# Four graph layers in one kernel: the attention layer in runs of two turns, PSUM as eight equal tiles, and closing steps per chunk

## Chip, cores and metric

The kernel runs on one core of a Trainium2 chip. The metric is the device time of one execution in microseconds (us); lower is better. The times are medians of several runs of the same program.

## What is computed

A graph of 4096 nodes with 64 features each, and a dense 0/1 matrix `adj` of 4096 x 4096, goes through four layers. Each has a layer norm and relu in front (`h`) and adds its result to `x`.

```python
# layer 0: weighted sums over neighbours, weights from a running count in each row of adj
x = x + (w(adj) @ (h @ W0) + b0)
# layer 1: attention masked by adj; q, k, s are "lorentz" linear maps of h
att = adj * sigmoid((2 + 2 * (qm @ k.T)) / att_scale + att_bias)
support = att @ s
x = x + support / sqrt(clip(abs(-inner(support)), 1e-8))
# layer 2: two gated steps (GRU), m = adj @ (g @ W)
r = sigmoid(i_r + h_r); z = sigmoid(i_z + h_z); n = tanh(i_n + r * h_n)
g = relu((1 - z) * n + z * g)
# layer 3: hyperbolic mean: num = adj @ (gamma * X), den = adj @ (gamma - 1),
# then scaling by tanh(alpha * 0.5 * artanh(|num / den|)), logmap, relu, expmap
```

## The kernel before

The nodes are cut into 32 blocks of 128 (`NB`), and the output nodes into four quarters `q` of 1024 (`NQ`), each of two halves `c` of 512 columns. `adj` is kept in SBUF in fp8, as tiles `A8[q][i]` for block pairs `i`. Each layer runs over the quarters, and inside a quarter over all 32 blocks, two blocks (one pair) to a turn.

**Order of the work.** Each engine executes its instructions in the order in which the program issues them. The streams of TensorE (`stream0`, `stream1`, `layer2`, `layer3`) are written out by hand. The small steps around them are Python generators (`post0`, `pre1`, `post1`, `post2a`, `post3` and others) that yield one instruction at a time. `Weave` holds a rough cost book of the engines; at each `weave.draw()` it issues those steps that should be ready by then, from the first two pieces of its list (`width`). `weave.until` and `weave.finish` issue steps until a result exists. `book_pe` is the planner's cost of a matmul; it charges a change between full and partial tiles of the array. All instructions of VectorE and ScalarE are issued by one helper, line 781, and all plain matmuls by line 976, so they are told apart here by the names of their tiles.

**PSUM.** There are four tiles of one bank (512 fp32 columns, `one`, line 820) and two of two banks (`two`, line 823). `weave.take` books a tile and `free` gives it back. Steps have an argument `kind` that says which of the two they use.

**Layer 1.** `weigh(q, i, c)` (line 1322) multiplies keys with queries for a pair of blocks and a half of 512 columns. The two blocks lie on the two halves of the partitions, so their score matmuls use array tiles of 64 x 128 side by side. One sigmoid of 1024 columns on ScalarE takes them from PSUM to a `sig` tile in SBUF (pool `b4`, six buffers, shared with the tiles `whole` of the check that `adj` has only zeros and ones). VectorE multiplies with the adjacency. `add` (in `stream1`, line 1345) sums over blocks with array tiles of 128 x 64 into two accumulators that live for a whole quarter. fp32 matmuls are recorded as two matmuls each, so two halves `c` of two blocks are eight records of scores and eight of sums to a turn. `stream1` issues the scores of turn i and then the sums of turn i - 1. In the first quarter it waits (`weave.until((1, ...))`) for the keys of each quarter, which `post0` and `pre1` of the last quarter still make. After the last sums of a quarter, `post1` takes its accumulators (`evac`: two copies `mt` on ScalarE, two adds on VectorE), transposes, normalises and makes the input of layer 2.

**Layer 3 and the end.** The output is made in eight chunks `u` of 512 nodes (four blocks, `CB`). `sum3` (line 1674) sums a chunk into two PSUM tiles, or one double tile in third place. `take3` (line 1737) copies it to `n65`. Chunks 0 to 2 get half their sums early, then 3 to 5 are completed, then 0 to 2, then 6 and 7 alone. `summed` (line 1729) starts `post3` for each three chunks together, and for 6 and 7 on their own. `post3` (line 1757) first has a group of seven steps for each chunk (sign, product, squares, `den`, sums of squares), then a chain of small steps for all chunks of the group, `artanh2` (line 1595) among them, and at its end the result `X` and its DMA. `preload` loads ScalarE's table for the next function ahead of its use.

Of the kernel before, what the change touches and what calls it, by code (L numbers as in the profile page):

```python
# [18 lines left out]
P = 128  # L19
D = 64  # L20
# [584 lines left out]
class Weave:  # L605
# [10 lines left out]
    def __init__(self):  # L616
        self.t = dict.fromkeys("PDAGS", 0.0)
        self.at, self.used = {}, {}
        self.banks = {1: [0.0] * 4, 2: [0.0] * 2}
        self.kind = {}  # L620
        self.work, self.back, self.width = [], [], 2
        self.late = 0.0
        self.quiet = False
        self.dma = 0.0
        self.busy = False
        self.table = None
        self.tiled = False
# [164 lines left out]
def fast_kernel(ctx: ExitStack, tc: tile.TileContext, t: dict, out: bass.AP, flag: bass.AP):  # L792
# [27 lines left out]
    def one(name):  # L820
        return weave.take(1, lambda: psp.tile([P, CW], F32, tag="one", name=name, bufs=4))

    def two(name):
        return weave.take(2, lambda: psp.tile([P, 2 * CW], F32, tag="two", name=name, bufs=2))

    def bank(kind, name):
        return one(name) if kind == 1 else two(name)[:, :CW]
# [136 lines left out]
    def book_pe(o, lhsT, rhs, passes):  # L964
        k, m, n = lhsT.shape[0], math.prod(lhsT.shape[1:]), math.prod(rhs.shape[1:])
        tiled = k < P or m < P
        dur = max(0.42e-3 * n * passes * (0.5 if tiled else 1.0) * (0.5 if k < P and m < P else 1.0), 0.09)
        if passes > 1 and not tiled:
            dur += 0.05 if passes == 2 else 0.075
        weave.book("P", dur + ((0.18 if passes == 4 else 0.115) if tiled != weave.tiled else 0.0), names(lhsT, rhs), names(o))  # L970
        weave.tiled = tiled
# [16 lines left out]
    def transpose4(src, kind, dst):  # L988

        def run():  # L990
            ps = bank(kind, "ps_t")
            for j in range(4):
                turn4(ps[:, j * P:(j + 1) * P], src[:, 2 * j:2 * j + 2, :].rearrange("p t d -> p (t d)"))
            return ps
        ps = yield PE([src], run, 0.6, [kind])
        yield AC.activation(dst, ps, AF.Copy)
        free(ps)

    def linear4(fm, weights, kind):

        def run():
            ps = bank(kind, "ps_l")
            for j in range(4):
                mm(ps[:, j * P:(j + 1) * P], fm[:, j * P:(j + 1) * P], weights)
            return ps
        return (yield PE([fm], run, 0.9, [kind]))
# [59 lines left out]
    def to_nm(a, kind):  # L1066

        def run():
            ps = bank(kind, "ps_n")
            for j in range(4):  # L1070
                turn4(ps[:, j * P:(j + 1) * P], a[:, j * P:(j + 1) * P])
            return ps
        ps = yield PE([a], run, 0.7, [kind])
        return blocks(ps)
# [30 lines left out]
    def checks():  # L1105
# [18 lines left out]
        def run():  # L1124
            ps = two("flag_ps")
            mm(ps[:1, :1], odds, ones)
            return ps
        ps = yield PE([odds], run, 0.3, [2])
# [3 lines left out]
    def stream0():  # L1132
# [56 lines left out]
        for q in range(NQ):  # L1189
            cnt[:] = [two(f"cnt{c}")[:, :CW] for c in (0, 1)]  # L1190
# [44 lines left out]
    def post0(q, acc):  # L1235
# [3 lines left out]
        ps = blocks((yield from linear4(a, w("w0"), 1)))  # L1239
# [31 lines left out]
    def pre1(q, X):  # L1271
# [5 lines left out]
        yield from transpose4(h, 1, fm)  # L1277
        hs = b2("hs")
        ps = yield from linear4(fm, w("w1"), 1)
# [6 lines left out]
        yield from transpose4(S1[q], 1, fm)  # L1286
# [19 lines left out]
        yield from transpose4(y, 1, kT[q])  # L1306
        DONE.add((1, q))
        qT = b2("qT", (P, CW))
        yield from transpose4(yq, 1, qT)
# [12 lines left out]
    def weigh(q, i, c):  # L1322

        kb = kT[i // 4][:, (i % 4) * P:(i % 4 + 1) * P]
        ps = two("score").rearrange("p (j n) -> p j n", j=2)
        for j in range(2):
            half = slice(j * D, (j + 1) * D)
            mm(ps[:, j, :], kb[half, :], qd[q][c][half, :])
        g = b4p.tile([P, 2, CW], F32, tag="b4", name="sig")
        S_.activation(g, ps, AF.Sigmoid, bias=att_add, scale=att_mul)  # L1330
        free(ps)
# [7 lines left out]
    def begin1():  # L1339

        for c in (0, 1):
            ahead.append(weigh(0, 0, c))
            weave.draw(False)

    def stream1():
# [11 lines left out]
        def add_behind():  # L1357
            q, i, gs = behind.pop()
            for c in (0, 1):
                add(c, q, i, gs)  # L1360
                weave.draw(weave.quiet)
            if i == NB // 2 - 1:
                weave.finish()
                weave.add(post1(q, acc[:], 1 if q < NQ - 1 else 2))
                acc.clear()

        for q in range(NQ):
            for i in range(NB // 2):
                if q == 0 and i % (QB // 2) == 0:
                    weave.until((1, i // (QB // 2)), DONE)  # L1370
                weave.quiet = (1, NQ - 1) not in DONE
                weave.late = 2.0 if weave.quiet else 1.0
                gs = ahead[:] if (q, i) == (0, 0) else []
                for c in range(len(gs), 2):
                    gs.append(weigh(q, i, c))
                    weave.draw(c == 1 or weave.quiet)
                if behind:
                    add_behind()
                behind.append((q, i, gs))
                if i == 8:  # L1380
                    load1(q + 1)
# [4 lines left out]
    def post1(q, acc, kind):  # L1386
# [4 lines left out]
        ps = yield from to_nm(a, kind)  # L1391
# [19 lines left out]
        yield from transpose4(g, kind, gT)  # L1411
# [82 lines left out]
    def load_gates(step):  # L1494
# [6 lines left out]
        def run():  # L1501
            ps = two("ps_g")
            mm(ps[:, :3 * D], m[:, :2 * D], m[:, 2 * D:])
            return ps
        ps = yield PE([m], run, 0.4, [2])
# [7 lines left out]
    def gates(q, step):  # L1513
# [4 lines left out]
        rz, ih = [None], [None]  # L1518
        assert ("gates", step) in DONE

        def news():

            ih[0] = two("ih")
            for c, (x, m) in enumerate(((lo, hi), (hi, lo))):
                o = lo if c == 0 else hi
                for own, half, i in ((x, 1, 2), (m, 0, 3)):
                    k = (4 * c + i) * D
                    mm(ih[0][o, half * CW:(half + 1) * CW], gw[own, k:k + D], mx[c][own, :])

        def gate(ps, half, i):  # L1530
            if ps[0] is None:
                ps[0] = two("rz")
            o = ps[0][:, half * CW:(half + 1) * CW]
            for c in (0, 1):
                k = (4 * c + i) * D
                mm(o[lo if c == 0 else hi, :], gw[:, k:k + D], mx[c])

        yield PE(mx, lambda: gate(rz, 0, 0), 0.9, [2, 2])
        yield PE(mx, news, 0.9, [2])
        r = b2("r", (P, CW))  # L1540
        yield AC.activation(r, rz[0][:, :CW], AF.Sigmoid, bias=gate_b[:, 2 * step:2 * step + 1])
        yield PE(mx, lambda: gate(rz, 1, 1), 0.9)
        yield DV.scalar_tensor_tensor(r, ih[0][:, CW:], gb[:, 5:6], r, op0=ALU.add, op1=ALU.mult)
        yield DV.tensor_tensor(r, r, ih[0][:, :CW], ALU.add)
        free(ih[0])
        z = b2("z", (P, CW))
        yield AC.activation(z, rz[0][:, CW:], AF.Sigmoid, bias=gate_b[:, 2 * step + 1:2 * step + 2])
        free(rz[0])
# [6 lines left out]
    def post2a(q):  # L1555
        x = yield from gates(q, 0)
        yield AC.activation(x, x, AF.Relu)
        ps = yield from to_nm(x, 1 if q < NQ - 1 else 2)
# [4 lines left out]
    def post2b(q):  # L1563
        o = yield from gates(q, 1)
        DONE.add(("gates", q))
        kind = 1 if q < NQ - 1 else 2

        def run():
            ps = bank(kind, "ps_o")
# [3 lines left out]
        ps = yield PE([o], run, 0.6, [kind])  # L1573
        yield DV.scalar_tensor_tensor(X[q], blocks(ps), 0.0, X[q], op0=ALU.max, op1=ALU.add)
        free(ps)
        yield from pre3(q, kind)
# [18 lines left out]
    def artanh2(x, between=()):  # L1595
# [4 lines left out]
        r = stat("at", nb)  # L1600
        yield DV.tensor_scalar(r, xc, -1.0, 1.0, op0=ALU.mult, op1=ALU.add)
        q = yield from recip(r)
        yield DV.scalar_tensor_tensor(q, xc, 1.0, q, op0=ALU.add, op1=ALU.mult)
        yield AC.activation(q, q, AF.Ln)
# [7 lines left out]
        for c in ARTANH_POLY[2:-1]:  # L1612
            yield DV.scalar_tensor_tensor(p, p, 2.0 * c, x2, op0=ALU.add, op1=ALU.mult)
        yield DV.scalar_tensor_tensor(p, p, 2.0 * ARTANH_POLY[-1], xc, op0=ALU.add, op1=ALU.mult)
# [6 lines left out]
    def pre3(q, kind):  # L1621
# [3 lines left out]
        yield from transpose4(hn, kind, fm)  # L1625
        ps = yield from linear4(fm, w("w3"), kind)
# [47 lines left out]
    def sum3(u, place, lo, hi):  # L1674

        if u not in dst:
            v = [two("acc3")] if place > 1 else [one("acc3") for _ in range(2)]
            dst[u] = lo, [x.rearrange("p (k n) -> p k n", n=256) for x in v]
        start, v = dst[u]
        for d in range(CB):  # L1680
            o = v[0][:, d, :W3] if len(v) == 1 else v[d // 2][:, d % 2, :W3]
# [45 lines left out]
    group = []  # L1727

    def summed(u, parts3, alone=False):
        group.append((u, parts3))  # L1730
        if alone or len(group) == 3:
            weave.add(post3(group[:]))
            group.clear()
# [23 lines left out]
    def post3(parts3):  # L1757
# [6 lines left out]
        sgn, den, ss = stat("sgn", nb), stat("den", nb), stat("ss", 2 * nb)  # L1764
        part = [slice(i * CB, (i + 1) * CB) for i in range(len(parts3))]
        vs = [n65[:, :, :D] for u, (n65, al) in parts3]
        for h, v, (u, (n65, al)) in zip(part, vs, parts3):
            d = n65[:, :, D]
            yield DV.tensor_scalar(sgn[:, h], d, 0.0, 2.0, op0=ALU.is_ge, op1=ALU.mult)
            yield DV.scalar_tensor_tensor(v, rows(sgn[:, h]), -1.0, v, op0=ALU.add, op1=ALU.mult)  # L1770
            sq = b2("sq")
            yield AC.activation(sq[:, :CB, :], v, AF.Square)
            yield DV.scalar_tensor_tensor(sq[:, CB:, :], v, 0.0, v, op0=ALU.max, op1=ALU.mult)
            yield DV.tensor_scalar(den[:, h], d, -1.0, DEN_EPS, op0=ALU.mult, op1=ALU.max)
            yield DV.tensor_tensor(den[:, h], den[:, h], d, ALU.max)
            yield DV.tensor_reduce(ss.rearrange("p (k b) -> p k b", k=2)[:, :, h],
                                   sq.rearrange("p (k b) d -> p k b d", k=2), AX.X, ALU.add)
# [124 lines left out]
```

## Time and profile before

| | |
|---|---|
| median of the runs shown | 809.76 us (808.28 to 809.77) |
| the profiled execution, in all | 808.12 us |
| its span, first to last instruction | 806.1 us |
| TensorE, share of the span with matmuls | 96% |
| VectorE / ScalarE / GpSimd busy | 79% / 49% / 8% |
| mean granted TensorE clock | 0.992 |
| layer 0 / layer 1 / layers 2 and 3 / after the last matmul | about 0-239 / 234-493 / 493-788 / 788-806 us |

Busy time of matmuls includes a modelled end, so that a full PE row means that nothing was seen to wait. The last number in brackets of a line is the idle time of the engine ahead of it, with the instruction that ended it. PE is TensorE's matmuls, PEld its weight loads, DVE VectorE, ACT ScalarE, POOL GpSimd and SP the queue of SyncE.

### The profile page before, as it was taken

How to read it: one execution, taken by the hardware profiler on the slowest of the kernel's cores; microseconds unless marked ns; L12 is line 12 of the kernel's file. 1: busy time of each engine (PE TensorE's matmuls, PEld its weight loads, DVE VectorE, ACT ScalarE, POOL GpSimd, SP SyncE). 2: the span in 40 equal slices, each digit the busy share in tenths (PEclk: the TensorE clock that was granted, in tenths of full speed). 3: DMA queues.
4: the chain of work that ended last, by engine and by line, in shares of the span. 5: the costliest groups of instructions: out<-in, count | busy, mean ns of one | idle time of the engine just before them, and what ended most of it. 6: DMA issues, size and time to landing. Idle time of an engine off the chain costs nothing. (4 is left out here: it accounts for less than half of the span.)

```text
span 806.1 us, 12128 instructions
## 1 busy us (share of the span) xinstructions
PE 772.6 (96%) x4494; PEld 360.1 (45%) x4494; DVE 635.6 (79%) x1429; ACT 397.8 (49%) x613; POOL 60.6 (8%) x125
## 2 busy tenths in 40 slices
PE   5999999999999999999999999999999999999991
PEld 2334444544443323333333333444444444599991
DVE  6886867877778798888888887878788777776696
ACT  5655555566556556667666664122220245444332
POOL 3332232231000000000000000000000000000000
PEclk9999999999999999999999999999999999999996
DMA  9999999999601032004022016597888600000010
GB/s 221 152 177 191 215 163 211 202 180 205 186 26 40 0 103 85 23 8 124 0 66 66 0 51 229 193 338 240 292 307 280 216 7 20 2 1 2 2 41 17
DMA packets 43955, 98.40 MB, mean 122 GB/s; under 512 B 5104, under 2 KB 20464, under 8 KB 43888
## 3 DMA queue, kind: packets, MB, share of 16 engines
q1 hardware_dynamic: 25888, 78.98, 29.0%
q0 software_dynamic: 15840, 14.42, 19.1%
q10 hardware_dynamic: 2160, 4.14, 1.4%
q8 instruction: 37, 0.61, 0.3%
q14 instruction: 30, 0.25, 0.1%
HBM read 135.54 MB, written 5.24 MB: 175 GB/s over the span
## 5 line engine op out<-in xcount | busy, mean ns | idle before, releaser
L781 ACT ACTIVATE sig<-score,fatt_add,fatt_mul 128x1024 f32<-128x1024 f32 x128 | 148.3, 1200 | 85.2 <-PE score L976 84.1
L781 DVE TENSOR_TENSOR sig<-sig,A 128x1024 f32<-128x1024 f32 x128 | 151.6, 1222 | 38.2 <-ACT sig L781 37.5
L781 DVE SCALAR_TENSOR_TENSOR whole<-whole 128x1024 f32<-128x1024 f32 x128 | 153.0, 1219 | 6.7 <-DMA whole<-in_adjT 6.1
L781 ACT ACTIVATE w<-cnt 128x512 int16<-128x512 f32 x198 | 111.6, 595 | 88.4 <-PE cnt L976 83.7
L976 PE MATMUL score<-qd,kT 64*128 64x512 f32 x512 | 128.2, 617 | 0.0
L976 PE MATMUL acc<-sig,S 128*64 128x512 f32 x512 | 125.4, 606 | 1.5 <-DVE sig L781 1.4
L976 PE MATMUL acc<-A,hm 128*128 128x512 fp8e4 x512 | 115.9, 379 | 0.0
L976 PEld LDWEIGHTS <-hm 128*128 128x128 bf16 x768 | 73.4, 98 | 91.3 <-issue 9.8
L976 PE MATMUL cnt<-A,ftri 128*128 128x512 fp8e4 x256 | 98.0, 386 | 8.1 <-ACT A L781 8.1
L976 PE MATMUL cnt<-A,fupd 128*128 128x512 fp8e4 x248 | 95.4, 385 | 3.4 <-ACT w L781 0.9
L976 PE MATMUL acc<-S,A 128*128 128x196 bf16 x1024 | 88.2, 246 | 0.2 <-DVE mx L781 0.2
L976 PEld LDWEIGHTS <-A 128*128 128x128 fp8e4 x1024 | 87.1, 96 | 1.5 <-issue 1.2
L976 PEld LDWEIGHTS score<-qd,kT 64*128 64x128 f32 x512 | 43.7, 186 | 80.9 <-ACT sig L781 39.1
L976 PE MATMUL acc<-w,hm 128*128 128x512 bf16 x256 | 75.6, 379 | 0.0
L781 DVE TENSOR_SCALAR w<-cnt 128x512 int16<-128x512 f32 x58 | 40.1, 691 | 39.4 <-PE cnt L976 38.2
L860 POOL DMA_DIRECT2D A<-in_adjT x110 | 58.8, 536 | 133.1 <-DMA A<-in_adjT 132.3
L976 PEld LDWEIGHTS acc<-sig,S 128*64 128x64 f32 x512 | 30.4, 136 | 82.7 <-issue 38.8
L976 PEld LDWEIGHTS <-lo 128*64 128x64 bf16 x768 | 39.3, 109 | 51.2 <-issue 22.5
L976 PE MATMUL acc<-A,lo 128*64 128x512 fp8e4 x512 | 59.4, 381 | 0.0
L781 ACT ACTIVATE mt<-acc 64x512 f32<-64x512 f32 x32 | 18.9, 591 | 66.0 <-PE acc L976 65.5
L976 PEld LDWEIGHTS <-ftri 128*128 128x128 bf16 x256 | 24.8, 98 | 47.2 <-issue 20.3
L1659 POOL MEMSET S<- 128x4 bf16 x8 | 0.9, 115 | 533.6 <-PE ps_l L976 463.2
(185 smaller groups left out, 631.5 us busy)
## 6 DMA issues: line engine op xcount, KB each, us to landing
whole<-in_adjT SPq DMA_DIRECT2D x128, 512.0 KB, 6.9
A<-in_adjT POOLq DMA_DIRECT2D x110, 128.0 KB, 14.0
qd<-qs SPq DMA_DIRECT2D x16, 128.0 KB, 4.1
mx<-gs SPq DMA_DIRECT2D x16, 128.0 KB, 7.8
xT<-gs SPq DMA_DIRECT2D x8, 256.0 KB, 7.2
x<-in_x SPq DMA_DIRECT2D x6, 256.0 KB, 6.2
xs<-x SPq DMA_DIRECT2D x4, 256.0 KB, 6.0
qs<-qT ACTq DMA_DIRECT2D x4, 256.0 KB, 6.0
```

Source lines behind the costliest of these rows:

```text
L781: return fn(*args, **kw)
L860: nc.gpsimd.dma_start(A8[q][b // 2][:, b % 2, :], a)
L976: nc.tensor.matmul(o, lhsT, rhs, start=start, stop=stop, skip_group_check=True)
L1659: nc.gpsimd.memset(S3[q, c][:, :, 3 * e:], 1.0)
```

## The change

In layer 1 `stream1` goes over pairs of turns: the scores of two turns are issued one after the other, then the sums of the two turns before (turn i - 1 and turn i). `weigh` is split: `score` issues the matmuls, `weigh` the sigmoids and the product. The sigmoid of a chunk becomes two instructions of 512 columns, one for each bank. For the second turn of a pair, `weigh` is put off (`later`) until the first turn's sums have been issued half by half.

PSUM becomes eight tiles of one bank. All users of double tiles take two or four single ones; `kind` goes away. The order and shape of their matmuls stay. The planner's book tells the shapes of partial tiles apart.

In the closing part, the first group of steps of a chunk becomes `head3` and is started as soon as each chunk of a group of three is taken; `post3` runs it for the last one alone. `artanh2` takes the difference of two logarithms in place of the logarithm of a quotient.

```diff
-        self.banks = {1: [0.0] * 4, 2: [0.0] * 2}
+        self.banks = {1: [0.0] * 8}
...
-        tiled = k < P or m < P
+        tiled = (k < P) + 2 * (m < P)
...
-    def weigh(q, i, c):
+    def score(q, i, c):
         kb = kT[i // 4][:, (i % 4) * P:(i % 4 + 1) * P]
-        ps = two("score").rearrange("p (j n) -> p j n", j=2)
+        ps = several(("score", "score"))
         for j in range(2):
             half = slice(j * D, (j + 1) * D)
-            mm(ps[:, j, :], kb[half, :], qd[q][c][half, :])
+            mm(ps[j], kb[half, :], qd[q][c][half, :])
+        return ps
+
+    def weigh(q, i, c, ps):
         g = b4p.tile([P, 2, CW], F32, tag="b4", name="sig")
-        S_.activation(g, ps, AF.Sigmoid, bias=att_add, scale=att_mul)
-        free(ps)
+        for j in range(2):
+            S_.activation(g[:, j, :], ps[j], AF.Sigmoid, bias=att_add, scale=att_mul)
+            free(ps[j])
...
-        def add_behind():
-            q, i, gs = behind.pop()
+        def add_behind(more=()):
+            q, i, gs = behind.pop(0)
             for c in (0, 1):
                 add(c, q, i, gs)
+                if more:
+                    more.pop(0)()
                 weave.draw(weave.quiet)
...
+        def turn(q, i, later=None):
...
+            gs = ahead[:] if (q, i) == (0, 0) else []
+            for c in range(len(gs), 2):
+                ps = score(q, i, c)
+                if later is None:
+                    gs.append(weigh(q, i, c, ps))
+                else:
+                    later.append(lambda q=q, i=i, c=c, ps=ps: gs.append(weigh(q, i, c, ps)))
+                weave.draw(weave.quiet or c == 1)
+            behind.append((q, i, gs))
...
         for q in range(NQ):
-            for i in range(NB // 2):
...
+            for i in range(0, NB // 2, 2):
+                later = []
+                turn(q, i)
+                turn(q, i + 1, later)
+                while len(behind) > 2:
+                    add_behind(later)
+                for go in later:
+                    go()
+                if len(behind) > 1:
                     add_behind()
...
-        yield PE(mx, lambda: gate(rz, 0, 0), 0.9, [2, 2])
-        yield PE(mx, news, 0.9, [2])
+        yield PE(mx, reset, 0.9, [1] * 4)
+        yield PE(mx, news, 0.9)
...
-        r = stat("at", nb)
-        yield DV.tensor_scalar(r, xc, -1.0, 1.0, op0=ALU.mult, op1=ALU.add)
-        q = yield from recip(r)
-        yield DV.scalar_tensor_tensor(q, xc, 1.0, q, op0=ALU.add, op1=ALU.mult)
-        yield AC.activation(q, q, AF.Ln)
+        q, r = stat("at", nb), stat("ln", nb)
+        yield AC.activation(q, xc, AF.Ln, bias=ones)
+        yield AC.activation(r, xc, AF.Ln, bias=ones, scale=-1.0)
...
+        yield DV.tensor_tensor(q, q, r, ALU.subtract)
...
     def sum3(u, place, lo, hi):
-            v = [two("acc3")] if place > 1 else [one("acc3") for _ in range(2)]
+            v = several(("acc3", "acc3"))
...
     def summed(u, parts3, alone=False):
+        if not group:
+            n = CB if alone else 3 * CB
+            group.append((stat("sgn", n), stat("den", n), stat("ss", 2 * n)))
         group.append((u, parts3))
+        i = len(group) - 2
+        if not alone and i < 2:
+            weave.add(head3(i, parts3, *group[0]))
+            heads.append(weave.work[-1])
+            return
+        for piece in heads:
+            while piece in weave.work:
+                weave.issue(piece)
+        heads.clear()
+        weave.add(post3(group[1:], *group[0]))
+        group.clear()
...
     def post3(parts3, sgn, den, ss):
-        for h, v, (u, (n65, al)) in zip(part, vs, parts3):
...
+        yield from head3(len(parts3) - 1, parts3[-1][1], sgn, den, ss)
         yield from preload(AF.Ln)
         rd = yield from recip(den)
         n, r = yield from lengths(ss)
```

`head3(i, part3, sgn, den, ss)` holds the seven steps of the removed loop for one chunk, unchanged, with `i` as the chunk's place in the group.

## The prediction

> **What bounds the kernel now.** I read the busy table first, then the slices by stage, then layer 1 in order of time, then the end.
>
> ```profile
> PE 772.6 (96%) x4494; PEld 360.1 (45%) x4494; DVE 635.6 (79%) x1429; ACT 397.8 (49%) x613; POOL 60.6 (8%) x125
> ...
> 234.00:292.00 58.00, 54.74 (x240) 18.45 (x238) 46.18 (x83) 32.82 (x36) 0.00 (x0) 1.00 0.09 28
> ...
> 292.00:491.00 199.00, 198.98 (x854) 63.28 (x853) 168.74 (x229) 132.16 (x129) 0.00 (x0) 1.00 0.18 55
> ```
>
> The columns of the two stretches are length, then PE, PEld, DVE, ACT, POOL. TensorE is busy without a gap from 292 to 491, which is layer 1 after its first turns; only the first stretch, 234 to 292, has about 3 us of idle PE. So in layer 1 the sum of PE time is the time. VectorE is at 85% (168.74 of 199) and ScalarE at 66%.
>
> ```profile
> 419.76 1.99 PE L976 MATMUL score<-qd,kT 64*128 64x512 f32 x8
> 421.68 1.94 PE L976 MATMUL acc<-sig,S 128*64 128x512 f32 x8
> 423.55 1.99 PE L976 MATMUL score<-qd,kT 64*128 64x512 f32 x8
> 425.46 1.94 PE L976 MATMUL acc<-sig,S 128*64 128x512 f32 x8
> 427.33 1.99 PE L976 MATMUL score<-qd,kT 64*128 64x512 f32 x8
> ...
> 420.30 0.19 PEld L976 LDWEIGHTS score<-qd,kT 64*128 64x128 f32 x2 [0.24 <-issue]
> 420.73 0.19 PEld L976 LDWEIGHTS score<-qd,kT 64*128 64x128 f32 x2 [0.23 <-issue]
> ...
> 424.78 2.38 ACT L781 ACTIVATE sig<-score,fatt_add,fatt_mul 128x1024 f32<-128x1024 f32 x2 [1.32 <-PE score L976]
> ...
> 426.02 2.40 DVE L781 TENSOR_TENSOR sig<-sig,A 128x1024 f32<-128x1024 f32 x2 [0.16 <-ACT sig L781]
> ```
>
> One turn, 423.55 to 427.33, takes 3.785 us. Within a shape, pairs of matmuls follow each other every 0.43 us (weight loads 420.30, 420.73). A turn has eight pairs, 3.44 us. The other **0.35 us** goes into two changes of tile shape, 64\*128 for the scores and 128\*64 for the sums.
>
> ```profile
> 744.80 43.51 PE L976 MATMUL acc<-S,A 128*128 128x196 bf16 x510
> ...
> 750.75 0.88 DVE L781 TENSOR_TENSOR n<-n,acc 128x260 f32<-128x260 f32 x2 [4.93 <-ACT alpha L781]
> ...
> 788.94 0.61 DVE L781 TENSOR_TENSOR n<-n,acc 128x130 f32<-128x130 f32 x2
> ...
> 793.24 0.42 DVE L781 SCALAR_TENSOR_TENSOR sq<-n 128x256 f32<-128x256 f32 x1
> ...
> 800.29 0.42 DVE L781 TENSOR_TENSOR X<-X,n 128x256 f32<-128x256 f32 x1
> ```
>
> At the end PE stops at 788.3 and VectorE carries the rest: the last chunk's sums lie in SBUF at 789.55, but its squares start only at 793.24, because the chunk before it (u=6) is still being closed. VectorE stood idle for 4.93 us ahead of 750.75 and is nearly full from there on.
>
> [...] The trace has 1200 ns for 1024 columns with two pointers [...] and 686 ns for z, 512 columns with one pointer [...]
>
> **Layer 1, what it removes.** 64 turns become 32 pairs: two turns of scores, then two of sums, four changes become two. 0.35 us a pair, 32 pairs: 11.2 us at most.
>
> **Layer 1, what it adds.** (1) A chunk's sigmoid becomes two instructions of 512 columns. Half a chunk costs 1200 - 512 x 0.833 = 774 ns (the slope also follows from 595 ns for w, 512 columns, and 170 ns for alpha, 2 columns). ACT gets 128 x (2 x 0.774 - 1.2) = 45 us more duration, of which overlaps hide some; it had 66 us free in 292-491 alone and stays under 85%. So not a bound by itself.
>
> (2) Two turns of scores want eight banks, but the accumulators hold two. The fourth chunk must reuse the first chunk's banks. Let a pair begin at 0. The first matmul after a change takes 0.10 more (693 against 589 ns), so pairs start at 0, 0.53, 0.96, ...; the fourth chunk is due at 2.68. ACT starts 1.23 after the first scores (424.78 - 423.55). Its two halves end at 1.23 + 0.67 + 0.77 = 2.67, 0.67 being 0.77 less the overlap of 0.10 (two sigmoids in 2.30 us). With some 0.05 to hand over (ACT to DVE: 425.98 to 426.02) that is 2.72, and weights that cannot be loaded ahead cost 0.10: a wait of **0.15 us**. Bounds: 0 if half a chunk costs half (600 ns), 0.25 if nothing overlaps. Queued behind the waiting load on PE are the rest of the scores and both sums, so all of it counts. Kept: 0.35 - 0.15 = 0.20 a pair.
>
> (3) The six b4 buffers: four sigmoid chunks live and two for the adjacency check. The third chunk's sigmoid is put behind the first sums of the turn before, which end near 4.9; the last half ends near 7.7, the next pair's first sigmoid is due at 7.4 + 1.23 = 8.6. Behind it wait only its own product and sums, 2 us later. Cost 0, covered by that 0.9 us of ACT. The products: the first turn's sums need them at 5.4 and 6.3, they are ready about 4.0 and 5.3; one check (1.22 us) in front eats most of this cover, so I keep 0 to 0.1 a pair here for the range.
>
> (4) Where q changes, the old accumulators stay until both adds have run (the second of them started at 316.30, about 5 us after those sums at 309.56-311.43), so scores have four banks for a pair. Chunk three then waits for chunk one, chunk four for chunk two: up to 1.4 us; none if the adds are out early. I take 0.7, three times: 2.1. Each q has two groups of transposes that hold a bank (ps_n from 320.92 to the end of its copy, 323.45): 0 to 0.3, I take 0.15, six times: 0.9. Half of these come to lie between two turns of scores, where they cause two more changes: three times 0.2, 0.6. Sum 3.6.
>
> (5) In the first q, PE waits for the keys of the last quarter: 1.79 us idle ahead of the ps_t at 291.17. Six pairs, 1.2 us, run into this wait; I count half, 0.6 (0 if the chain of small steps does not move up, and it can lose 2 us if its steps queue behind longer runs of scores).
>
> Layer 1: 26 pairs x 0.20 = 5.2, + 0.6 - 3.6 = **2.2 us gained**; bounds -5 and +9.
>
> **PSUM in equal tiles elsewhere.** Same banks and same matmuls, so no PE time. A third-place unit is taken in two pieces, not one: 0.3 us more on DVE (four adds of 0.29 for two of 0.43), three times, off the path while PE runs to 788.3. Gates need four free banks at once, as they needed both double tiles. No DMA or queue entry is added; loads (SP) keep their place. Checks not done in a shorter layer 1 move to layer 2; the last one ran at 636.8, far from the end.
>
> **Closing steps.** The first step group of a chunk (sign, product, square, den, sums) is about 1.87 us of DVE (751.56 to 753.43). Today three such run together after the third chunk. Two of each three move ahead, the first two (3.7 us) into the 4.93 idle us before 750.75. Then the group 3, 4, 5 is out of the way near 765 and gives room for the next two. Group 0, 1, 2 starts at about 769.3, with one step group instead of three, and closes near 779 instead of 784.3. Chunk 6 is in SBUF at 779.0; it takes 1.9 + 5.8 us, done near 787, before chunk 7 at 789.55. So chunk 7 squares at about 790.2 instead of 793.24: **3.0 us**. Artanh: three small DVE steps and a Ln go (r, reciprocal, product: 0.2 each), one subtract and a Ln of 0.2 us on ACT come: 0.4 us less on DVE. ACT's table for tanh also loads earlier, since both Ln start right from the clipped value (796.78), ending about 0.4 sooner than 797.80. Together **3.5 us**, bounds 2 and 4.5.
>
> **Sum.** 2.2 + 3.5 = 5.7. The profiled execution had a span of 806.1 and 808.12 us in all; it lies 1.6 below the median of the runs shown, 809.76. I carry the difference over: 809.76 - 5.7 = 804.
>
> **Rivals.** A, the scores' banks cost nothing: halves fast enough and old accumulators gone. Layer 1 gives 9 to 10, all 13: **797**. For it: PE shows no bank wait today. Against: 774 ns for a half.
>
> B, the switches are saved, but waits for banks at the fourth chunk and at changes of q eat all: only the end gains, **806 to 808**. For it: my own margin is negative by 0.15.
>
> C, slower: **ScalarE becomes the pacer of the fourth chunk.** If the first chunk's second half ends 0.45 later (a side step of 0.6 us between, or a late start), each pair waits 0.60: 32 x 0.60 = 19.2 against 11.2 + 3.5: **814**. It decides from 0.46 us a pair. For it: every half has its own wait now. Against: of ACT's 132.16 us in 292-491 the sigmoids are 126 (52.5 turns x 2.4), so side work is 6 us only.
>
> D, slower too: the last quarter's gates in layer 3 (rz at 699.33) find three banks instead of four and wait for the first take at 710. The quarter is ready at 737 and used near 739, so up to 8 us of PE wait: **812**. For it: small margin. Against: today's double tiles are as scarce there.
>
> That shapes do not alternate less is excluded, since PE runs in program order.
>
> **Chances.** Forecast 0.40, A 0.22, B 0.20, C 0.10, D 0.08. B straddles the limit of 0.2% (1.6 us, about what a measurement of this kernel can tell from no change), and parts of C and D and of the forecast's low end meet there: faster 0.63, within 0.13, slower 0.24. The range 796 to 813 reaches from A to D and leaves most of C out. The forecast's own range is 800 to 808.
>
> **What would show it.** Right: score groups of 16 matmuls in a row, then sums of 16; a pair of turns near 7.4 us instead of 7.57; a half sigmoid near 770 ns; small PE waits on ACT at the fourth chunk; and 9 us instead of 12.4 from PE's end to the last X. Wrong: pairs of 7.22 (A) or above 7.6 (C), PE idle ahead of the last quarter in layer 3 (D), or the last chunk still squared 5 us after PE's end.

## The result, and the profile after

The changed kernel takes **806.82 us** (median of 13 runs, 806.41 to 807.29) against 808.22 us for the kernel before in the same comparison (13 runs, 807.83 to 809.77): ratio 0.9975, 95% interval 0.9967 to 0.9983 (the two medians alone give 0.9983). It is faster, by 1.4 us and not by 5.7. The kernel before has two groups of times, near 808.1 and near 809.6 us, for which the last section has a likely cause; its profiled execution (808.12) belongs to the first, so the stages below are compared with that one. The changed kernel's profiled execution took 807.01 us, span 805.1, mean clock 0.993.

Where the time went, from the first score, the first sums of layer 2 and of layer 3, and the end of the last matmul in each trace (us). The quarters of layer 1 run from first score to first score, the tail from the last matmul to the last output `X`:

| | layer 0 | q0, q1, q2, q3 of layer 1 | layer 1 | layer 2 | layer 3 | tail |
|---|---|---|---|---|---|---|
| before | 234.0 | 73.7, 61.7, 61.7, 63.8 | 261.0 | 199.4 | 93.9 | 12.4 |
| after | 234.2 | 70.5, 63.4, 63.5, 65.1 | 262.5 | 198.4 | 95.5 | 9.0 |

The tail gave the 3.4 us that it should. Layer 1, where 2.2 were to be gained, lost 1.5, and layer 3 lost 1.6.

The busy table of after, and its two stretches of layer 1 (length, then PE, PEld, DVE, ACT, POOL, clock):

```profile
PE 767.5 (95%) x4473; PEld 369.7 (46%) x4494; DVE 635.6 (79%) x1419; ACT 432.2 (54%) x756; POOL 61.6 (8%) x125
```

```profile
234.00:292.00 58.00, 56.73 (x257) 22.27 (x256) 48.73 (x88) 40.61 (x63) 0.00 (x0) 1.00 0.11 36
292.00:491.00 199.00, 192.63 (x832) 68.39 (x830) 172.87 (x236) 153.16 (x226) 0.00 (x0) 1.00 0.21 66
```

The stretch that was full before (198.98 of 199) now has 6.4 us of idle TensorE: there is less matmul time to do, and it is waited for. ScalarE is at 77%. An undisturbed pair, in the timeline (start, duration):

```profile
329.47 3.79 PE L973 MATMUL score<-qd,kT 64*128 64x512 f32 x16
333.19 3.65 PE L973 MATMUL acc<-sig,S 128*64 128x512 f32 x16
336.77 3.79 PE L973 MATMUL score<-qd,kT 64*128 64x512 f32 x16
...
330.63 2.79 ACT L781 ACTIVATE sig<-score,fatt_add,fatt_mul 128x512 f32<-128x512 f32 x4 [0.83 <-PE score L973]
334.31 2.79 ACT L781 ACTIVATE sig<-score,fatt_add,fatt_mul 128x512 f32<-128x512 f32 x4 [0.90 <-PE acc L973]
```

From 329.47 to 336.77 are 7.30 us, where two turns took 7.57: the saved changes are there. But not every pair looks like this. The waits of ScalarE and of the weight loads (us in total, times, longest) in after:

```profile
PEld acc L973 <- DVE sig L781: 26.1, 42, 1.8
...
ACT sig L781 <- DVE whole L781: 25.2, 18, 2.3
```

A sigmoid waits for `whole`, the adjacency check on VectorE, with which it exchanges no data. What they share is the pool `b4`. Before, this row had 0.8 us in three waits. One of the 18 in order of time:

```profile
361.83 1.22 DVE L781 SCALAR_TENSOR_TENSOR whole<-whole 128x1024 f32<-128x1024 f32 x1
...
362.98 1.22 DVE L781 SCALAR_TENSOR_TENSOR whole<-whole 128x1024 f32<-128x1024 f32 x1
...
364.12 1.22 DVE L781 TENSOR_TENSOR sig<-sig,A 128x1024 f32<-128x1024 f32 x1
364.31 4.13 ACT L781 ACTIVATE sig<-score,fatt_add,fatt_mul 128x512 f32<-128x512 f32 x6 [2.30 <-DVE whole L781]
...
365.40 1.08 PE L973 MATMUL acc<-sig,S 128*64 128x512 f32 x4 [0.35 <-DVE sig L781]
365.79 3.90 DVE L781 TENSOR_TENSOR sig<-sig,A 128x1024 f32<-128x1024 f32 x3 [0.44 <-ACT sig L781]
...
367.06 1.08 PE L973 MATMUL acc<-sig,S 128*64 128x512 f32 x4 [0.58 <-DVE sig L781]
```

The second check ends at 364.21 with its accumulator read, the sigmoid starts at 364.31, 2.30 us after ScalarE was free. TensorE waits twice. The first wait, 0.35 us, is for the product at 364.12; its sigmoids had ended at 362.01, and it stood behind the two checks on VectorE. The second, 0.58 us, is for the product at 365.79, that of the late sigmoid. These 16 sums take 4.96 us instead of 3.58.

At the end of the kernel:

```profile
791.03 0.61 DVE L781 TENSOR_TENSOR n<-n,acc 128x130 f32<-128x130 f32 x2 [1.27 <-ACT alpha L781]
...
792.66 0.42 DVE L781 SCALAR_TENSOR_TENSOR sq<-n 128x256 f32<-128x256 f32 x1
...
799.20 0.43 DVE L781 TENSOR_TENSOR X<-X,n 128x256 f32<-128x256 f32 x1
```

TensorE stops at 790.62. The last chunk is squared 2.0 us later (before: 4.9), and VectorE even waits 1.27 us for it; from the square's start to the end of X are 7.0 us (before: 7.5).

### The profile page after: what moved, and what is told of

It reads as the page before. It is cut to its first block, busy times and chain, and to the rows that moved or that the text cites. A ratio compares the mean times of both kernels' runs of the same rounds, so it can differ in the third digit from the quotient of the medians.

```text
span 805.1 us, 12309 instructions
## 1 busy us (share of the span) xinstructions
PE 767.5 (95%) x4473; PEld 369.7 (46%) x4494; DVE 635.6 (79%) x1419; ACT 432.2 (54%) x756; POOL 61.6 (8%) x125
## 4 chain that ended last, share of the span: by engine, by line
PE 80%; DVE 9%; ACT 6%; issue 2%; DMA 1%; SPq 0%; ACTq 0%; DVEq 0%
PE acc L973 50%; PE cnt L973 13%; PE score L973 10%; ACT sig L781 5%; DVE sig L781 3%; DVE whole L781 2%; PE rz L973 2%; PE ps_l L973 2%; DMA whole<-in_adjT 1%; PE ps_t L977 1%; PE ih L973 1%; ACT w L781 1%; DVE ss L781 1%; PE ps_kq L973 1%; DVE w L781 1%
## 5 line engine op out<-in xcount | busy, mean ns | idle before, releaser
L781 ACT ACTIVATE sig<-score,fatt_add,fatt_mul 128x512 f32<-128x512 f32 x256 | 179.2, 779 | 57.1 <-DVE whole L781 25.2
L781 DVE TENSOR_TENSOR sig<-sig,A 128x1024 f32<-128x1024 f32 x128 | 154.9, 1223 | 29.9 <-ACT sig L781 25.5
L973 PE MATMUL score<-qd,kT 64*128 64x512 f32 x512 | 126.3, 612 | 1.5 <-ACT sig L781 1.5
L973 PE MATMUL acc<-sig,S 128*64 128x512 f32 x512 | 120.2, 601 | 4.2 <-DVE sig L781 3.9
L973 PEld LDWEIGHTS score<-qd,kT 64*128 64x128 f32 x512 | 50.5, 186 | 72.0 <-issue 46.7
L973 PE MATMUL acc<-w,hm 128*128 128x512 bf16 x235 | 70.6, 379 | 0.9 <-issue 0.2
L973 PEld LDWEIGHTS acc<-sig,S 128*64 128x64 f32 x512 | 32.5, 136 | 83.5 <-issue 40.8
```

What stands on the lines that cost most here:

```text
L781: return fn(*args, **kw)
L973: nc.tensor.matmul(o, lhsT, rhs, start=start, stop=stop, skip_group_check=True)
```

## The experiments

The texts on record name their theories anew each time. That the buffers tie sigmoids to late checks is "theory A" in those of e3 and e4, where "theory B" is the PSUM banks, and "theory B" in those of f1 to f3. "Theory C" is that VectorE simply has too much to do in layer 1. "Checks" are those of the adjacency, 23 of which run in layer 1 of after. All twelve kernels were timed against the kernel before on the same chip. Its medians there are 809.2 to 809.5 us, as more of its runs fell in its upper group, so that for this alone these ratios can lie about 0.001 below the 0.9975 above. The stages, which don't depend on that, are:

| kernel | median us, ratio [95%] | q0, q1, q2, q3 | layer 1 | layer 2 | layer 3 | tail |
|---|---|---|---|---|---|---|
| e4 pairs, 24 checks left out | 797.61, 0.9856 [0.9841, 0.9871] | 69.3, 60.3, 60.3, 63.0 | 252.9 | 199.0 | 95.5 | 9.0 |
| e2 single turns | 806.47, 0.9966 [0.9952, 0.9980] | 71.3, 61.7, 63.0, 65.9 | 262.0 | 198.7 | 95.5 | 9.0 |
| f1 before, checks later | 815.61, 1.0088 [1.0074, 1.0102] | 73.7, 61.7, 61.7, 63.8 | 261.0 | 199.6 | 95.9 | 16.9 |
| f2 single turns, checks later | 807.01, 0.9977 [0.9969, 0.9986] | 71.4, 61.7, 61.7, 64.2 | 259.0 | 198.2 | 94.2 | 14.0 |
| f3 pairs, checks later | 800.71, 0.9902 [0.9887, 0.9916] | 69.3, 60.3, 60.3, 63.0 | 252.9 | 198.2 | 94.2 | 14.0 |
| e3 checks at fixed places | 811.89, 1.0031 [1.0021, 1.0042] | 69.3, 60.2, 66.1, 71.4 | 267.1 | 198.7 | 95.5 | 9.0 |
| e1 before, closing edits | 813.78, 1.0053 [1.0040, 1.0067] | 75.3, 61.7, 61.7, 63.8 | 262.6 | 203.1 | 97.9 | 9.0 |
| g1 before, two logarithms | 814.97, 1.0070 [1.0057, 1.0084] | 75.3, 61.7, 61.7, 63.8 | 262.6 | 203.1 | 97.9 | 11.7 |
| g2 after, one logarithm | 806.39, 0.9969 [0.9958, 0.9981] | 70.6, 63.4, 63.5, 65.0 | 262.5 | 198.4 | 94.1 | 10.0 |
| f4 f3, third quarter's pre3 later | 804.74, 0.9945 [0.9932, 0.9959] | 69.3, 60.3, 60.3, 63.0 | 252.9 | 198.2 | 100.5 | 12.1 |
| h1 two checks a quarter | 797.60, 0.9857 [0.9842, 0.9872] | 69.3, 60.3, 62.6, 63.0 | 255.2 | 198.2 | 93.8 | 9.0 |
| h2 four checks a quarter | 796.21, 0.9842 [0.9829, 0.9856] | 69.3, 60.9, 60.3, 62.9 | 253.4 | 198.5 | 93.5 | 9.0 |

### Checks out of layer 1: e4_checks_left_out

```diff
         todo = [(b, q) for n, (q, b) in enumerate(tiles) if not direct(n)]
+        todo = todo[:-24]
...
-        return self.work[:self.width] + ([] if self.quiet else self.back)
+        return self.work[:self.width] + ([] if self.quiet or self.hold else self.back)
...
+    weave.hold = True
     stream1()
+    weave.hold = False
```

> The changed kernel without the 24 adjacency checks that fall into layer 1 (left out altogether: 24 of 128 tiles are not checked). Theory A (buffers): as with checks at a fixed point, layer 1 about 253 us. Theory C (VectorE is simply too full, 24 checks of 1.3 us are 31 us of its time): layer 1 gets shorter here, to 253 or less, but stays near 262 where the checks are only placed elsewhere. Theory B (banks): 261 or more here too.

Layer 1 takes 252.9 us instead of 262.5, and no sigmoid waits for a check. So the checks cost the pairs 9.6 us, but this alone does not tell buffers from VectorE's load.

### One turn at a time: e2_single_turns

```diff
-            for i in range(0, NB // 2, 2):
-                later = []
-                turn(q, i)
-                turn(q, i + 1, later)
-                while len(behind) > 2:
-                    add_behind(later)
-                for go in later:
-                    go()
+            for i in range(NB // 2):
+                turn(q, i)
                 if len(behind) > 1:
                     add_behind()
```

> The changed kernel with stream1 in single turns again (scores of one turn, then sums of the turn before); eight PSUM tiles, sigmoids of 512 columns and closing steps stay. Theory A (the pairs save switches and lose more by waits for sig buffers): layer 1 goes back to about 261 us from 262.5, span 803.6. Theory B (the split sigmoids or the equal PSUM tiles cost the time, the pairs gain): layer 1 gets longer by the switches, 264 us or more, span 807 or more. In both the last matmul to the last X stays at 9.0 us and layer 3 keeps its 1.6 us of idle PE.

With the checks in place, single turns take 262.0 us and pairs 262.5: **the pairs as changed gain nothing**. That is neither the 261 of theory A nor the 264 of theory B. The wait for checks is here too, 13.0 us in 21 waits.

### The same, checks done in layer 2: f1, f2, f3

Only `hold` of e4's diff, on before (f1), on e2 (f2) and on after (f3). Nothing is left out; the checks run after layer 1.

> The kernel before, with the adjacency checks held back during layer 1 and done in layer 2 (nothing is left out). Theory B (a late check holds a buffer that a sigmoid needs; this bites only with the changed kernel's tighter use of the buffers): before waited only 0.8 us for checks in layer 1, so layer 1 stays at 260 to 261 us and the whole within 1.5 us of before. Theory C (VectorE is loaded too heavily in layer 1, whatever the buffers): before would gain too, some 3 to 8 us. If layer 2 cannot take the checks, layer 2 gets longer than 200 us.

> The changed kernel with turns one at a time (scores of one turn, sums of one) and the checks held out of layer 1. Theory B: with buffers free, what remains over the pairs is only the changes of tile shape: 16 turns of 3.785 us a quarter, layer 1 at 259 to 261 us, 6 to 8 us longer than the pairs with checks later (32 x 0.27 = 8.6 less the pairs' own waits). If the pairs gain nothing by themselves, and the gain of leaving out the checks was all VectorE's time, layer 1 here is near 253 too.

> The changed kernel with pairs, all checks of layer 1 moved to layer 2; nothing is left out. Theory B: layer 1 at 253 us as with the checks left out, layer 2 at 198 to 200 (VectorE has some 43 of 199 us free there, 24 checks take 30), layer 3 at 95.5 with the 1.6 us wait at ps_o: 797 to 799 in all, ratio 0.985 to 0.987. If the checks only move their cost: layer 2 longer by up to 10 us, 806 to 808.

Layer 1 by itself answers the question:

| layer 1, us | checks in it | checks later | price of the checks |
|---|---|---|---|
| before (single turns, sigmoids of 1024) | 261.0 | 261.0 | 0.0 |
| single turns, sigmoids of 512, eight tiles | 262.0 | 259.0 | 3.0 |
| pairs | 262.5 | 252.9 | 9.6 |

The gain of the pairs is 6.1 us without checks and none with them. What I had as "cost 0" is as large as the whole gain. The three kernels have 17, 29 and 23 checks in layer 1, so the price does not follow their number. Before did not mind its checks at all: there, the load of VectorE as such (theory C) does not bound. For the pairs h2, below, shows it.

The matmuls of layer 1 come in the same order in after and in f3, so that one can see where after falls behind. 1.3 of the 9.6 us are products that stood behind checks on VectorE (0.29, 0.52 and 0.52 us, ahead of the three changes of quarter). The other 8 or so follow sigmoids that waited for a buffer, in part by way of PSUM: behind each change the transposes `ps_n` wait 0.69 to 0.81 us for a bank that such a sigmoid frees late, and the next scores lose 0.9 us while ScalarE catches up.

The totals of f1 and f3 are worse than was expected, by some 5 and 2 us. About ten checks were not done in layer 2 either and were forced in layer 3, in a row, where the first group of three chunks begins to close. VectorE in f3:

```profile
729.80 1.22 DVE L781 SCALAR_TENSOR_TENSOR whole<-whole 128x1024 f32<-128x1024 f32 x1
...
740.79 1.23 DVE L781 SCALAR_TENSOR_TENSOR whole<-whole 128x1024 f32<-128x1024 f32 x1
```

They take 12.2 us; the first X of that group is out at 765.2 us, and the tail is 14.0 instead of 9.0. In f1 the last check ended after 751 us and its tail is 16.9. Checks are free in layer 2, and ten of them in layer 3 are dear; five in h1, the last of which ends at 737.1, left the tail at 9.0.

### Checks at fixed places: e3_checks_placed

After's checks are held back in layer 1, and one is issued by hand between the scores of the two turns of each pair from the third pair on, six a quarter.

```diff
                 turn(q, i)
+                if i > 2:
+                    check()
                 turn(q, i + 1, later)
```

> The changed kernel, in layer 1 with each adjacency check issued at one point only, once a pair from i = 4 on: after the product of the pair's first turn, when all other b4 buffers are in use, so that its buffer goes back to the next check and not to a sigmoid. As many checks as in the changed kernel, about six a quarter. Theory A (sigmoids wait for buffers that a late check still holds): the 3.1 us of waits in each of the quarters 1 to 3 go, layer 1 about 253 us instead of 262.5, ScalarE's waits for whole near 0 instead of 25 us, span about 796. Theory B (PSUM banks are what the scores and sums wait for): layer 1 stays at 261 or more.

In q1 it is as good as without checks (60.2 us), with six of them there, and only one sigmoid still waited. But `post1` paid for it: its last product `g` starts 69.7 us after the first score of q1, in f3 after 40.2. And q2 and q3 got 5.8 and 8.4 us longer. Waits in e3:

```profile
PE ps_t L977 <- DVE g L781: 10.1, 3, 4.6
...
ACT sig L781 <- DVE whole L781: 2.5, 1, 2.5
```

The checks ran ahead of `post1`'s steps, and `g` came late; the transposes of `g` had been issued to TensorE by then, and with them everything behind them in its queue waited, three times, up to 4.6 us. Of the 5.8 and 8.4 us, 1.7 and some 3 are a lowered clock behind these gaps (last section). I had cured one wait and made another.

### The closing edits apart: e1, g1 and g2

e1 is the kernel before with `artanh2`, `head3`, `summed` and `post3` of the changed one, g1 only with its `artanh2`; g2 is the changed kernel with the old `artanh2`. The edit of g1:

```diff
-        r = stat("at", nb)
-        yield DV.tensor_scalar(r, xc, -1.0, 1.0, op0=ALU.mult, op1=ALU.add)
-        q = yield from recip(r)
-        yield DV.scalar_tensor_tensor(q, xc, 1.0, q, op0=ALU.add, op1=ALU.mult)
-        yield AC.activation(q, q, AF.Ln)
+        q, r = stat("at", nb), stat("ln", nb)
+        yield AC.activation(q, xc, AF.Ln, bias=ones)
+        yield AC.activation(r, xc, AF.Ln, bias=ones, scale=-1.0)
...
+        yield DV.tensor_tensor(q, q, r, ALU.subtract)
```

> The kernel before with the closing part alone (head3 per chunk, artanh by two logarithms), PSUM tiles and layer 1 as before. Theory (the end gains by itself what it gained in the whole change): from the last matmul to the last X 9.0 us instead of 12.4, span 802.7, that is 3.4 under the 806.1 of before; layer 1 stays at 261.0 us from the first scores to the first sums of layer 2. Rival (the end gains only because layer 3 was shifted by the rest of the change): 11 us or more from the last matmul to the last X.

> The kernel before with only artanh2 changed to two logarithms. The closing edits alone (e1) made layer 2 3.7 us and layer 3 4.0 us longer, by waits of the gates (rz behind r). head3 runs only in layer 3, so artanh2, which pre3 uses too, should be what moves layer 2: layer 2 at 203, layer 3 at 94 to 98, the tail about 0.4 below 12.4, in all 811 to 815. If layer 2 stays at 199.4, the cause in e1 is elsewhere.

> The changed kernel with the old artanh2 (logarithm of the quotient). Layer 1 unchanged at 262.5. The tail 0.4 us longer (9.4), as I had put the two logarithms at 0.4. Layer 3: if the stall of 1.6 us at ps_o comes from the order of the logarithm and tanh of pre3 between the last r and z, it can go (94) or stay (95.5) with this kernel; 806 to 808.5 in all.

e1 has the whole gain of the tail (9.0) and is slower than before. g1 shows why: it has the same longer layers 2 and 3 (203.1 and 97.9) with `artanh2` alone. `artanh2` is used by `pre3` too. With other costs in the planner's book, `pre3` of a quarter and the gates of the next are interleaved in another order. e1's TensorE and ScalarE there:

```profile
677.62 0.59 PE L976 MATMUL acc<-A,hm 128*128 128x512 fp8e4 x2
680.46 1.08 PE L976 MATMUL rz<-mx,g 128*64 128x512 f32 x4 [2.24 <-ACT r L781]
```

```profile
677.82 0.60 ACT L781 ACTIVATE h3T<-ps_t 128x512 f32<-128x512 f32 x1 [6.26 <-PE ps_t L980]
678.42 1.28 ACT L781 ACT_TABLE_LOAD   x1
679.72 0.69 ACT L781 ACTIVATE r<-rz,gate_b 128x512 f32<-128x512 f32 x1
```

The gate r is read by ScalarE only behind `h3T` and a table load, and the matmuls of z wait 2.24 us, since in the old PSUM r and z are halves of one double tile. The table load takes 1.28 us here, and the next instruction starts 0.02 us after its end. The changed kernel, whose r and z are separate tiles, has no such wait, nor the one of 0.62 us that before had at 549.8; that is 0.6 of the 1.0 us that layer 2 gained; the other 0.4 stays open.

What it has in place of it is the stall of 1.6 us in layer 3. ScalarE and TensorE in after:

```profile
703.07 0.69 ACT L781 ACTIVATE r<-rz,gate_b 128x512 f32<-128x512 f32 x1
...
707.54 0.30 ACT L781 ACTIVATE at<-axc,fones 128x8 f32<-128x8 f32 x1 [1.75 <-DVE axc L781]
...
709.57 1.28 ACT L781 ACT_TABLE_LOAD   x1
710.86 0.69 ACT L781 ACTIVATE z<-rz,gate_b 128x512 f32<-128x512 f32 x1
...
718.93 0.63 PE L977 MATMUL ps_o<-fident,xT 128*128 128x128 f32 x4 [1.63 <-DVE xT L781]
```

Between the last quarter's r and z lie the logarithms of the third quarter's `pre3` with their table loads, 7.8 us in all; so `xT` is late. In f3, with the same gates and the same `pre3`, z was issued right behind r, and nothing waits:

```profile
691.13 0.69 ACT L781 ACTIVATE r<-rz,gate_b 128x512 f32<-128x512 f32 x1
691.72 0.68 ACT L781 ACTIVATE z<-rz,gate_b 128x512 f32<-128x512 f32 x1
```

With the old `artanh2` (g2) layer 3 is at 94.1 and the tail at 10.0, where I had expected 9.4. The two logarithms gain 1.0 us in the tail and lose 1.4 here: g2 and after are within 0.5 us of each other.

### The third quarter's entry later: f4_pairs_later_gates

```diff
         o = yield from gates(q, 1)
+        if q == NQ - 1:
+            weave.add(pre3(q - 1))
         DONE.add(("gates", q))
...
-        yield from pre3(q)
+        if q != NQ - 2:
+            yield from pre3(q)
```

> As f3, and the third quarter's entry into layer 3 (pre3, with its Ln and tanh) is started only behind the last quarter's gates. Theory: the 1.6 us of TensorE's wait at ps_o in layer 3 goes away, layer 3 at 94 us, 795.5 to 797.5 in all, 1.6 below f3. Rival: the third quarter's input of layer 3 is then late itself, and the wait comes back at its sums (no gain, or up to 3 us lost).

A miss. f3 had no stall to cure, and the third quarter's `S` became late: TensorE waits 3.5 us for it, and layer 3 takes 6.3 us longer.

### A few checks where nothing is pending: h1 and h2

As f3, with e3's `check()` under another condition: only while no step of `post1` is pending (h1, eight checks in layer 1), or at four turns (h2, 14 checks):

```diff
                 turn(q, i)
+                if i in (0, 10, 12, 14):
+                    check()
                 turn(q, i + 1, later)
```

> The changed kernel; in layer 1 a check is issued only between the scores of the two turns of a pair, and only when no step of post1 is pending (two for each quarter, 8 in all); the other checks run in layer 2. Nothing is left out. Theory: the sigmoids keep their buffers, layer 1 stays near 253 to 254.5 us, and with 77 instead of 85 checks left only about 2 fall into layer 3 instead of 10, so that the tail after the last matmul is 9 to 10.5 us instead of the 14.0 of f3. In all 796 to 799, below f3 (800.7). If the tail of f3 has another cause than its late checks, it stays at 14 and the whole at 800.

> As h1 with four checks a quarter at fixed places (turns 0, 10, 12 and 14; 14 in all), two of them inside the last steps of post1. Theory: no check is left for layer 3 (tail 9.0), but if a check ahead of post1's last product delays the transposes as in e3, each such quarter costs 2 to 5 us: layer 1 at 253 to 256 without that, 260 or more with it; 796 to 800, or above 803.

h2 is the fastest of all with nothing left out: **796.21 us, ratio 0.9842**, 10.6 us below the changed kernel. Its stretches of layer 1:

```profile
234.00:292.00 58.00, 56.73 (x255) 21.97 (x254) 46.88 (x83) 41.52 (x65) 0.00 (x0) 1.00 0.07 23
292.00:488.00 196.00, 194.23 (x854) 69.42 (x853) 170.54 (x229) 156.30 (x231) 0.00 (x0) 1.00 0.18 55
```

VectorE is as full as in after (87% of its stretch in both), and TensorE's idle time is 1.8 us instead of 6.4: at this load VectorE keeps up, which speaks against theory C. One sigmoid waits for a check, 1.98 us at 354.45, in q1, which takes 60.9 us instead of 60.3. h1 has fewer checks, one of which is in a bad place:

```profile
370.15 1.44 ACT L781 ACTIVATE sig<-score,fatt_add,fatt_mul 128x512 f32<-128x512 f32 x2 [2.50 <-DVE whole L781]
```

That wait lies just ahead of the old accumulators' copies, and its quarter, q2, takes 62.6 us instead of 60.3. So eight checks cost layer 1 2.3 us, and 14 cost 0.5: it is the place of a check that counts, not the number. Inside a quarter a wait of this length costs little (0.6 us in h2, nothing in q1 of e3, where it was 2.5). All this fits the theory of the buffers. Its direct test, more `b4` buffers, was not tried.

## Why the prediction was right or wrong

**The step that failed** is (3), "The six b4 buffers: four sigmoid chunks live and two for the adjacency check ... Cost 0, covered by that 0.9 us of ACT." I set the buffers against the sums that free them, in a pair without side work, and took the two others as the checks' own. But all six are handed out in turn from one pool. A sigmoid often gets the buffer that a check had last, and then must wait until VectorE has run that check, behind its products, however early ScalarE is ready. Price: 262.5 - 252.9 = **9.6 us**, shown by f3 and, with checks in layer 1, by h2. I allowed "0 to 0.1 a pair" for a check in front of products, at most 3.2 us. That cost was there too, 1.3 of the 9.6.

**A second error hid part of it.** Without the checks' waits, layer 1 gained 8.1 us, not 2.2:

- A pair saves 0.27, not 0.20. The half sigmoid is 779 ns (I had 774). But the bank wait at the fourth chunk is 0.08, not 0.15: ScalarE starts 1.16 us after the pair begins and its second half ends at 2.61, where I had 1.23 and 2.67. 24 pairs outside the first quarter: 6.5 against 4.8.
- Changes of quarter and transposes: I took 3.6. Without checks q1, q2 and q3 gained 1.4, 1.4 and 0.8, where eight pairs each would give 2.2: 2.9 lost. About right.
- The first quarter: I took 0.6 and 0.4 for its two other pairs; it gained 4.4, of which 2.3 come with single turns already (f2). The wait of 1.79 us for the keys at 289.4 is gone, not halved. How much of this the half sigmoids and how much the free banks bring was not separated.

Sum: 6.5 - 2.9 + 4.4 = 8.0, against 8.1 measured; this is a division of the measured gain and no test of it. With the 9.6 for the checks, that is the 1.5 us lost.

**The tail** was right: 3.5 predicted, 3.4 measured, in after and in e1 alike. Its parts were less so. The last chunk is squared 2.9 us sooner after TensorE's end (predicted 3.0), and from square to X it takes 0.5 less (predicted 0.4). But with the old logarithm (g2) the square is 0.45 us later too, since chunk 6 is closed later: the logarithms bring 1.0 in all (0.7 where they are the only change, g1), and `head3` some 2.4 instead of 3.0.

**Moved steps.** I counted `artanh2` by its own instructions and only in the closing part. It also runs in `pre3`, in the middle of layers 2 and 3, where a changed cost in the planner's book changes the order on ScalarE: 1.4 us in the changed kernel (after against g2), and 7.7 in the old PSUM (g1), lowered clock included. "Same banks and same matmuls, so no PE time" was wrong in the good direction: separate tiles for r and z took a wait of 0.6 us away, and others in e1.

**The rivals.** B gives the right total with the wrong cause: buffers ate the gain, and banks only passed the wait on. C was wrong as a rate: ScalarE is at 77% and keeps up with every undisturbed pair; the scores wait for it only where a check has made it late. D named the place of layer 3's loss, but no bank is short there. A's 797 is what the kernel reaches once the checks are moved (h2: 796.2), but by another sum: layer 1 gains 7.6 us there, not 9 to 10.

**The base.** The 809.76 that I subtracted from is in the upper group of the kernel before; its profiled execution, from which all terms came, is in the lower. From 808.12 the sum gives 802.4; that 804 lies 1.6 us nearer to the result is luck.

## To carry to other kernels

A pool shared by two engines' work ties them together: a tile waits for the last reader of the buffer that it happens to get, so that low-priority work with a late reader can hold up the critical chain without exchanging any data with it. When a change makes a stage tighter, look again at everything that was free in it because of slack, first at shared buffers. Side work is best placed where what waits behind it has slack: here inside a quarter, and neither ahead of a chain that TensorE's queue waits for (e3) nor just ahead of a change of quarter (h1). And a change to a small function is costed at all its callers, by the order that it makes and not by its instructions alone.

## What the runs showed of the hardware

A gap in TensorE's work of about 2 us can cost as much again. e1 is longer than before by 3.7 and 4.0 us in layers 2 and 3, but its waits at r are only 2.24 and 2.08. The rest is the granted clock (PEclk, third figure from the end). Behind the gap in the first quarter, and behind the gap of 2.24 us at 678, in e1:

```profile
291.20:295.20 4.00, 3.97 (x16) 1.75 (x16) 2.80 (x5) 2.02 (x3) 0.00 (x0) 0.68 0.32 59
680.40:684.40 4.00, 3.94 (x16) 2.25 (x17) 1.44 (x2) 1.10 (x4) 0.00 (x0) 0.67 0.00 0
684.40:688.40 4.00, 4.00 (x24) 1.69 (x24) 3.27 (x14) 3.96 (x7) 0.23 (x2) 0.90 0.00 0
```

The same stretch of the kernel before, behind a gap of the same 1.79 us:

```profile
291.20:295.20 4.00, 3.97 (x20) 1.83 (x22) 3.15 (x6) 2.71 (x4) 0.00 (x0) 1.00 0.31 63
```

At 0.67 and 0.90 for 4 us each, 4 x 0.33 + 4 x 0.10 = 1.7 us of matmul time are lost. By the clocks of two slices of 4 us that begin where a gap ends, the gaps of the traces compare as follows:

| gap ahead of (us), length | clock of the two slices | matmul time lost |
|---|---|---|
| e1 680.46, 2.24 | 0.67, 0.91 | 1.7 |
| e1 707.90, 2.08 | 0.65, 0.92 | 1.7 |
| g1 680.74, 2.24 | 0.60, 0.97 | 1.7 |
| g1 708.13, 2.08 | 0.59, 0.99 | 1.7 |
| e3 373.43, 4.58 | 0.57, 1.00 | 1.7 |
| e3 439.33, some 4 | 0.50, 0.76 | 3.0 |
| f4 728.20, 3.53 | 0.50, 0.83 | 2.7 |
| e1 291.10, 1.78 | 0.70, 0.88 | 1.7 |
| g1 291.48, 1.8 | 0.62, 0.96 | 1.7 |
| before 291.17, 1.79 | 1.00, 1.00 | 0 |
| f1 291.47, 1.8 | 1.00, 1.00 | 0 |
| f1 752.25, 1.94 | 1.00, 1.00 | 0 |
| after 718.93, 1.63 | 1.00, 1.00 | 0 |

All seven gaps of 2.08 us and more were followed by a lowered clock, and the one of 1.63 us was not. Of the five from 1.78 to 1.94 two were and three were not; what tells these apart was not shown. The first 16 us of a run, where before has gaps of 5.76 and 2.32 us, are not in this comparison.

This would also account for the two groups of times of the kernel before, 1.5 us apart, if its gap of 1.79 us is followed by a lowered clock in some executions and not in others: the same gap was in e1 and g1, at a cost of 1.7 us, and was not in f1 and in the profile of before, an execution of the lower group. Of its 54 runs in the four comparisons 31 are in the upper group. Where runs have a clock on record, it is 0.989 to 0.990 in the upper group and 0.991 to 0.992 in the lower; 1.7 us of 806 are 0.002. There is no profile of an upper run, so that this last link is inferred. The changed kernel no longer has that gap, and its 13 runs lie within 0.9 us.
